# Two stacked cross-attention layers: where the last output projections stand, and in which order the first unit is set up

## The chip, the cores and the metric

The kernel runs on one core of one Trainium2 chip. The metric is the device time of one execution, in microseconds (us). A core has a matrix engine, TensorE (PE in the profile; its weight loads are the rows PEld), VectorE (DVE), ScalarE (ACT), GpSimd (POOL) and SyncE (SP). DMA transfers are issued by instructions on SP's and ACT's queues and run beside the engines. Matrix products go from SBUF to PSUM[...].

## The reference

x is 32 batches of 256 tokens with 320 channels, the context 32 batches of 77 tokens with 512 channels. Two layers run one after the other; each has 20 heads of 16 channels and adds its result to its input. The reference has more branches for context tokens beyond the 77th, but there are none, so each layer is, with weights and a bias of its own:

```python
q = heads(x @ wq); k = heads(ctx @ wk); v = heads(ctx @ wv)
p = softmax(q @ k.T / 4)          # over the 77 context tokens
x = x + merge(p @ v) @ wo + bias
```

Everything is float32.

## The kernel before

**Units.** Two batches make a pair; a *unit* is one pair in one layer, so there are 32 units. `units_in_order` starts layer 0 four pairs ahead of layer 1 and then alternates; the last four units are pairs 12 to 15 in layer 1. Data lie with channels on partitions: a tile of 128 x 1280 holds channels 0 to 127 and 128 to 255 of both batches (1024 columns) and, in the last 256 columns, the remaining 64 channels of both batches, one batch above the other. A unit is cut into five *groups* of heads and batches (`of_group`); groups 0 to 3 are a channel block and a batch, group 4 is the rest of both.

**Steps of a unit**, with the tile that the profile shows for each. Each product is written in column strips of 32 (`by_columns`, line 173).
- `keys`, `keys_rest` (psk, lines 230 and 248): context times key weights; ACT copies the result to kR (lines 245, 263), and `mask_keys` (line 219, POOL) makes two versions kT, one for each head of a pair. `less_keys` (line 226, POOL) makes kM, which also carries a row that subtracts the maximum.
- `queries`, `queries_rest` (psq, lines 266 and 278): x times query weights; ACT copies to q0 (lines 276, 284). `queries_rest` also issues a DMA that copies all of q0 to q1 (line 285, 640 KB).
- `maxima` (psm, line 335): query times key, only to get each row's maximum; DVE reduces four banks (line 343).
- `turn` (line 350): DVE transposes the maxima of all groups to mT, and eight small DMAs on SP's queue (line 356) write them into q0 and q1, into rows that belong to the other head. Scores then come out with the maximum subtracted.
- `scores` (pss, line 369), exponentials on ACT (pT, line 375, four of 590 ns a group).
- `values` (po, line 389): the numerators and, from columns of ones, the sums. DVE transposes (line 401) and takes reciprocals (405), POOL multiplies (410), DVE transposes back into oT (`turn_back`, line 424).
- `finish`, `finish_rest` (psy, lines 437 and 445): oT times output weights; `add` (line 431, DVE) adds bias and residual into the x tile. `main_channels` covers the 256 channels, `last_channels` the remaining 64; the rest is for output channels 256 to 319. In layer 1 the x tile is then stored (line 452; for the last unit group by group, line 435).
- `vals`, `place_vals` (psv, lines 293 and 311): values in chunks of 128 context rows, placed per unit by DMA (line 322).

**Order.** The order is written out by hand. `at(slot, where, step)` puts steps into *slots*, five per unit; unit u's scores stand in slots 5u to 5u + 4. Within a slot the order is load, maxima, turn, scores, values, rest, back, full, last (line 506). Unit u prepares itself beside the scores of the units before it: context loaded in slot 5u − 12, queries in 5u − 9, keys in 5u − 8, values from 5u − 6, maxima in 5u − 6 to 5u − 2, turn in 5u − 2; it finishes in 5u + 6 and 5u + 8 (lines 462 to 496). For the last two units `finish` and `finish_rest` stand in slots 159 and 160. Slots below 0 are the prologue. Every engine and every DMA queue keeps to the program's order; what waits for what is by semaphores. PSUM banks are handed out in rotation, eight of them, so a step waits for the reader of the bank that was handed out eight banks earlier.

**Prologue.** At the start SP's queue loads unit 0's context and then pair 0's x, ACT's queue the key weights and then the query weights of layer 0 (lines 134 to 137). TensorE's first step is `keys(0)`, then `queries(0)`.

Of the kernel before, what the change touches and what calls it, by code (L numbers as in the profile page):

```python
# [48 lines left out]
F32 = mybir.dt.float32  # L49
# [19 lines left out]
PARTS, WIDE = {}, 0  # L69
# [21 lines left out]
def xattn_kernel(ctx: ExitStack, tc: tile.TileContext, xT, cT, cP, weights, outT):  # L91
    nc = tc.nc
# [3 lines left out]
    work = ctx.enter_context(tc.tile_pool(name="work", bufs=3))  # L96
# [3 lines left out]
    units = units_in_order()  # L100
    NU = len(units)

    def bank(name):
        return psum.tile([P, 512], F32, tag="bank", name=name)

    xs, cs, cvs = {}, {}, {}

    def load_x(p):
        x_sb = io.tile([P, NX], F32, tag="x", name=f"x_{p}", bufs=AHEAD + 3)
        nc.sync.dma_start(out=x_sb, in_=xT[p])  # L110
        xs[p] = x_sb

    def load_context(u):
        p = units[u][0]
        c_sb = cs[u] = io.tile([P, NKA, NB * L], F32, tag="c", name=f"c_{u}", bufs=3)
        nc.sync.dma_start(out=c_sb, in_=cP[:, p])


    w_sb = []
# [7 lines left out]
    def load_weights(layer, first, last, queue):  # L127
        a = PARTS[first][0]
        at, rows, width = PARTS[last]
        b = at + rows * width  # L130
        queue.dma_start(out=w_sb[layer]["all"][:, a:b], in_=weights[layer][:, a:b])


    load_context(0)
    load_weights(0, "k", "k", nc.scalar)
    load_x(0)
    load_weights(0, "q", "q22", nc.scalar)

    ident = const.tile([P, P], F32, name="ident")
    make_identity(nc, ident)  # L140
# [19 lines left out]
    masks = const.tile([P, 2], F32, name="masks")  # L160
# [3 lines left out]
    for e in range(2):  # L164
        i = HD * (1 - e)
        nc.vector.tensor_scalar_mul(less[:, e : e + 1], r32[:, i : i + 1], -1.0)

    st = [{} for _ in units]

    def by_columns(out, lhsT, rhs, **flags):  # L170

        for m in range(0, out.shape[0], 32):
            nc.tensor.matmul(out[m : m + 32], lhsT[:, m : m + 32], rhs, **flags)  # L173
# [6 lines left out]

    def last_channels(ps, w2, x, **flags):
        for t in range(2):
            for b in range(NB):
                r = slice(64 * b, 64 * b + 64)
                by_columns(
                    ps[t][b][:, 0:S], w2[r, 0, t * P : (t + 1) * P], x[r, 2 * NT : NX], **flags
                )

    def main_channels(ps, w, x, start, stop):
        for t in range(2):
            for kc in range(2):
                for b in range(NB):
                    i = kc * NT + b * S
                    by_columns(
                        ps[t][b][:, 0:S], w[:, kc, t * P : (t + 1) * P], x[:, i : i + S],
                        start=(start and kc == 0), stop=(stop and kc == 1),
                    )

    def project_rest(ps, w, w22, x):

# [12 lines left out]
    def mask_keys(u, g0, g1):  # L215

        kR, kT = st[u]["kr"], st[u]["k"]
        for e in range(2):
            nc.gpsimd.tensor_scalar_mul(kT[:, e, g0:g1], kR[:, g0:g1], masks[:, e : e + 1])  # L219

    def less_keys(u):

# [43 lines left out]
    def queries(u):  # L266
        p, layer = units[u]
        w = w_sb[layer]
        q0, _ = st[u]["q"] = [
            work.tile([P, NX], F32, tag=f"q{e}", name=f"q{e}_{u}", bufs=3) for e in range(2)  # L270
        ]
        ps = [[bank(f"psq_{u}_{t}_{b}") for b in range(NB)] for t in range(2)]
        last_channels(ps, w["q2"], xs[p], start=True, stop=False)
        main_channels(ps, w["q"], xs[p], start=False, stop=True)
        for g in range(4):
            nc.scalar.copy(of_group(q0, g), ps[g // 2][g % 2][:, 0:S])  # L276

# [72 lines left out]
    def turn(u):  # L350
        mT = work.tile([P, 2 * NG * 32], F32, tag="mT", name=f"mT_{u}", bufs=2)
        nc.vector.transpose(mT, maxes[u % 2].rearrange("p k i -> p (k i)"))
        for e in range(2):
            q = st[u]["q"][e].rearrange("(j i) n -> i j n", i=32)[HD * (1 - e)]
            for a in range(P // 32):
                nc.sync.dma_start(  # L356
                    out=q.rearrange("j (k a n) -> a j k n", a=P // 32, n=32)[a],
                    in_=mT[32 * a + e : 32 * a + 8 : 2].rearrange("j (k n) -> j k n", n=32),
                )
# [17 lines left out]
    def products(u, g):  # L377
        vpad = st[u]["v"]
        if "o" not in st[u]:
            st[u]["o"] = work.tile([P, NX], F32, tag="oT", name=f"oT_{u}", bufs=2)  # L380
        po = bank(f"po_{u}_{g}")
        pT = st[u].pop(("p", g))
        for e in range(2):
            for j in range(4):
                if g < 4:
                    b, pair = g % 2, 4 * (g // 2) + j
                else:
                    b, pair = j // 2, 8 + j % 2
                nc.tensor.matmul(  # L389
                    po[32 * j : 32 * j + 32, e * S : (e + 1) * S],  # L390
                    vpad[:L, b, pair, e].rearrange("p a d -> p (a d)"),
                    pT[j][:L, e * S : (e + 1) * S],
                    start=True,
                    stop=True,
                )
        return po
# [21 lines left out]
    def values(u, g):  # L418
        st[u]["n", g] = divide(u, g, products(u, g))
# [7 lines left out]
    def add(u, g, ps):  # L427
        p, layer = units[u]
        x = of_group(xs[p], g)
        t = g // 2  # L430
        nc.vector.scalar_tensor_tensor(  # L431
            x, ps[:, 0:S], w_sb[layer]["b"][:, 0, t : t + 1], x, ALU.add, ALU.add
        )
        if u == NU - 1:
            nc.sync.dma_start(out=of_group(outT[p], g), in_=x)

    def finish(u):
        w = w_sb[units[u][1]]
        ps = [[bank(f"psy_{u}_{t}_{b}") for b in range(NB)] for t in range(2)]
        main_channels(ps, w["o"], st[u]["o"], start=True, stop=False)  # L440
        last_channels(ps, w["o2"], st[u]["o"], start=False, stop=True)
        for g in range(4):
            add(u, g, ps[g // 2][g % 2])

    def finish_rest(u):
        p, layer = units[u]
        w = w_sb[layer]
        ps = bank(f"psy_{u}_2")
        project_rest(ps, w["o"], w["o22"], st[u]["o"])
        add(u, 4, ps)  # L450
        if layer == 1 and u < NU - 1:
            nc.sync.dma_start(out=outT[p], in_=xs[p])
        st[u].clear()


    place = {}
# [1 line left out]
    def at(slot, where, step):  # L458
        place.setdefault((slot, where), []).append(step)

    made = [0, 0]
    for u, (p, layer) in enumerate(units):
        s = NG * u
        if layer == 0 and u > 0:
            at(s - 14, "load", lambda p=p: load_x(p))
        if u > 0:
            at(s - 12, "load", lambda u=u: load_context(u))
        at(s - 8 if u else s - 9, "rest", lambda u=u: keys(u))
        at(s - 9, "last", lambda u=u: queries(u))
        at(s - 7, "rest", lambda u=u: keys_rest(u))  # L470
# [12 lines left out]
        for g in range(NG):  # L483
            at(s - 6 + g, "maxima", lambda u=u, g=g: maxima(u, g))
# [3 lines left out]
        at(s - 2, "turn", lambda u=u: turn(u))  # L488
        if u < NU - 2:
            at(s + NG + 1, "full", lambda u=u: finish(u))  # L490
            at(s + NG + 3, "rest", lambda u=u: finish_rest(u))
        else:

            slot = NG * NU - (u == NU - 2)
            at(slot, "full", lambda u=u: finish(u))
            at(slot, "last", lambda u=u: finish_rest(u))


    at(-10, "load", lambda: load_weights(0, "v", "v", nc.scalar))
# [106 lines left out]
```

## Time and profile before

| | |
|---|---|
| time, median of 3 runs | 984.96 us (984.57 to 988.63) |
| the profiled execution's own time | 986.19 us |
| its span, first to last instruction | 984.4 us |
| TensorE busy | 968.2 us, 98% of the span |
| DVE, ACT, POOL busy | 566.7, 430.1, 240.9 us |
| DMA | 83.59 MB, mean 85 GB/s |
| mean granted TensorE clock | 0.995 |

A row of a timeline gives start, duration, engine, line and operation, written and read tiles, the shape, the count of instructions, and in brackets how long the engine had been idle before it and what ended that. A float32 product appears as two instructions, so a maxima step of 8 products is x16. Durations of grouped rows overlap with the next row, since products are pipelined; the distance from one start to the next is what a step takes. A row of a stretch gives its bounds, its length, the busy time and count of PE, PEld, DVE, ACT and POOL, then the granted TensorE clock (1.00 is full), the share of the DMA engines in use and GB/s.

### The profile page before, as it was taken

To read this page: it belongs to the slowest core of one execution; us is meant where nothing else is said; L and a number is where in the kernel's file an instruction comes from. 1 tells how busy PE (TensorE), PEld (TensorE's weight loads), DVE (VectorE), ACT (ScalarE), POOL (GpSimd) and SP (SyncE) were. 2 spreads that over 40 slices of the span, in tenths; PEclk is the share of its full clock that TensorE was granted. 3 is DMA by queue.
4 is the path that set the end of the run, shared out by engine and by line. 5 is a ranking of instruction groups with operands and counts; after the bars stand their busy time and mean duration, and the time that the engine had idled before them with its cause. 6 is when DMAs were issued, how large, how long until landed. Compare 5 with 4: busy or idle time off the path is not lost.

```text
span 984.4 us, 43943 instructions
## 1 busy us (share of the span) xinstructions
PE 968.2 (98%) x19664; PEld 597.3 (61%) x19664; DVE 566.7 (58%) x1316; ACT 430.1 (44%) x937; POOL 240.9 (24%) x364
## 2 busy tenths in 40 slices
PE   7899999999999999999999999999999999999988
PEld 4566665666665666665666666666656666656644
DVE  2466555665555655556655556655556655556554
ACT  1354444444444444444544444543444444444443
POOL 3132221322212322212312213322223222123211
PEclk9999999999999999999999999999999999999999
DMA  6450222212132311323212232311323122231111
GB/s 216 165 174 21 92 80 97 70 62 72 64 123 71 121 54 50 107 81 123 63 51 85 70 124 71 104 44 60 123 81 118 33 67 70 70 108 48 50 57 55
DMA packets 53949, 83.59 MB, mean 85 GB/s; under 512 B 15556, under 2 KB 35652, under 8 KB 53762
## 3 DMA queue, kind: packets, MB, share of 16 engines
q1 hardware_dynamic: 53330, 78.96, 24.0%
q8 instruction: 154, 2.52, 1.0%
q10 hardware_dynamic: 432, 1.84, 0.5%
q14 instruction: 33, 0.27, 0.1%
HBM read 35.39 MB, written 10.49 MB: 47 GB/s over the span
## 4 chain that ended last, share of the span: by engine, by line
PE 97%; DMA 1%; DVE 1%; SPq 1%; POOL 0%; issue 0%; ACT 0%; DVEq 0%; POOLq 0%
PE po L389 16%; PE psy L173 15%; PE psq L173 15%; PE pss L369 14%; PE psm L335 12%; PE psv L173 9%; PE psk L173 7%; PE psq L212 4%; PE psy L212 4%; PE psk L256 2%; SPq L356 1%; DMA w<-in_w_dram 1%; DVE max L343 0%; DMA q<-mT 0%; POOL kT L219 0%
## 5 line engine op out<-in xcount | busy, mean ns | idle before, releaser
L375 ACT ACTIVATE pT<-pss 77x512 f32<-77x512 f32 x640 | 326.8, 590 | 210.4 <-PE pss L369 210.4
L343 DVE TENSOR_REDUCE max<-psm 128x4 f32<-128x308 f32 x640 | 260.6, 469 | 197.4 <-PE psm L335 194.0
L410 POOL TENSOR_TENSOR normal<-turned,inv 128x256 f32<-128x256 f32 x160 | 99.2, 620 | 684.5 <-DVE inv L405 684.5
L369 PE MATMUL pss<-q,kM 32*77 32x256 f32 x2560 | 170.9, 377 | 4.5 <-DMA q<-mT 4.5
L389 PE MATMUL po<-pT,v 77*32 77x256 f32 x2560 | 173.1, 388 | 1.3 <-DVE max L343 1.3
L173 PE MATMUL psy<-oT,w 128*32 128x256 f32 (+1 forms) x3072 | 149.2, 380 | 0.0
L173 PE MATMUL psq<-x,w 128*32 128x256 f32 (+1 forms) x3072 | 149.2, 379 | 0.0
L276 ACT COPY q<-psq 128x256 f32<-128x256 f32 x128 | 47.6, 372 | 205.9 <-PE psq L173 202.1
L401 DVE STREAM_TRANSPOSE turned<-po 128x512 f32<-128x512 f32 x160 | 113.3, 708 | 38.4 <-PE po L389 35.4
L424 DVE STREAM_TRANSPOSE oT<-normal 128x256 f32<-128x256 f32 x160 | 71.3, 445 | 109.4 <-POOL normal L410 109.4
L335 PE MATMUL psm<-kT,q 32*128 32x154 f32 x2560 | 129.4, 314 | 1.2 <-POOL kT L219 1.2
L335 PEld LDWEIGHTS psm<-kT,q 32*128 32x128 f32 x2560 | 92.2, 183 | 57.0 <-issue 34.9
L389 PEld LDWEIGHTS po<-pT,v 77*32 77x32 f32 x2560 | 67.4, 109 | 89.9 <-DVE max L343 58.7
L173 PEld LDWEIGHTS psq<-x,w 128*32 128x32 f32 (+1 forms) x3072 | 85.4, 108 | 57.2 <-issue 13.6
L173 PEld LDWEIGHTS psy<-oT,w 128*32 128x32 f32 (+1 forms) x3072 | 82.2, 109 | 61.2 <-issue 13.2
L369 PEld LDWEIGHTS pss<-q,kM 32*77 32x77 f32 x2560 | 102.2, 142 | 24.5 <-issue 6.8
L219 POOL TENSOR_SCALAR kT<-kR,masks 128x77 f32<-128x77 f32 (+1 forms) x128 | 96.7, 766 | 50.9 <-ACT kR L245 41.3
L431 DVE SCALAR_TENSOR_TENSOR x<-psy,w,x 128x256 f32<-128x256 f32 x160 | 68.6, 479 | 61.2 <-PE psy L173 56.5
L173 PE MATMUL psv<-w,cv 128*32 128x320 f32 x1232 | 93.5, 433 | 0.0
L173 PE MATMUL psk<-c,w 128*32 128x154 f32 x2048 | 75.0, 298 | 5.8 <-DMA w<-in_w_dram 5.8
L173 PEld LDWEIGHTS psk<-c,w 128*32 128x32 f32 x2048 | 67.0, 111 | 12.9 <-DMA w<-in_w_dram 5.8
L173 PEld LDWEIGHTS psv<-w,cv 128*32 128x32 f32 x1232 | 41.1, 110 | 40.6 <-issue 2.2
(25 smaller groups left out, 349.1 us busy)
## 6 DMA issues: line engine op xcount, KB each, us to landing
q<-q SPq DMA_DIRECT2D x32, 640.0 KB
x<-in_xT_dram SPq DMA_DIRECT2D x16, 640.0 KB
c<-in_cP_dram SPq DMA_DIRECT2D x32, 308.0 KB
cv<-in_cT_dram SPq DMA_DIRECT2D x38, 256.0 KB
out_dram<-x SPq DMA_DIRECT2D x15, 640.0 KB
v<-stage SPq DMA_DIRECT2D x26, 192.5 KB
q<-mT SPq DMA_DIRECT2D x256, 5.0 KB
w<-in_w_dram ACTq DMA_DIRECT2D x2, 640.0 KB
```

What stands on the lines that cost most here:

```text
L173: nc.tensor.matmul(out[m : m + 32], lhsT[:, m : m + 32], rhs, **flags)
L212: nc.tensor.matmul(ps[r, 0:S], lhsT, rhs, start=(kc == 0), stop=(kc == 2))
L219: nc.gpsimd.tensor_scalar_mul(kT[:, e, g0:g1], kR[:, g0:g1], masks[:, e : e + 1])
L335: nc.tensor.matmul(ps[j][:, c * 2 * L : (c + 1) * 2 * L], q[r, c * P : (c + 1) * P], kT[r, :, g, :], start=True, stop=True,)
L343: nc.vector.tensor_reduce(mx[:, 2 * g : 2 * g + 2, 2 * j : 2 * j + 2], ps[j][:, : 4 * L].rearrange("p (c e k) -> p c e k", e=2, k=L), AX.X ...
L369: nc.tensor.matmul(ps[j][:L, e * S : (e + 1) * S], kM[r, e, g, :], q[r, :], start=True, stop=True,)
L375: nc.scalar.activation(st[u]["p", g][j][:L], ps[j][:L], AF.Exp, scale=SCALE)
L389: nc.tensor.matmul(po[32 * j : 32 * j + 32, e * S : (e + 1) * S], vpad[:L, b, pair, e].rearrange("p a d -> p (a d)"), pT[j][:L, e * S : (e ...
L401: nc.vector.transpose(turned[:, 0 : 2 * S], po)
L410: nc.gpsimd.tensor_tensor(normal.rearrange("p q e d -> p e q d"), outs, inv.unsqueeze(3).broadcast_to([P, 2, S // 32, HD]), ALU.mult,)
L424: nc.vector.transpose(of_group(st[u]["o"], g), normal)
L431: nc.vector.scalar_tensor_tensor(x, ps[:, 0:S], w_sb[layer]["b"][:, 0, t : t + 1], x, ALU.add, ALU.add)
```

## The change

In the tail, the output projections of units 28, 29 and 30 are held back. Each `finish` is split into two halves, one for each 128 output channels, and the halves and rests get slots of their own: unit 28 in 151, 152 and (rest) 148, unit 29 in 153, 154 and 155, unit 30 in 156, 159 and 157. A half uses two banks in place of four and runs the last channels first. The store of a unit follows its last part. Unit 31 finishes in slot 160 as before. oT gets three buffers in place of two.

In the prologue the loads of pair 0's x (in three pieces) and of the query weights (in three) come ahead of those of the context and the key weights, and TensorE's first step is `queries(0)` with the last channels last, then `keys(0)` and its rest. Ahead of it stand five products of the identity with itself, whose result nobody reads. Unit 0's key masks go from POOL to DVE. Unit 0's maxima stand in slots −6, −5, −4, −4 and −3, its turn in −3 with two of its eight DMAs on ACT's queue; keys and queries of unit 1 move to slots −4 and −3. Pair 1's x is loaded on ACT's queue.

```diff
+        if p == 0:
+            for a, b in ((0, NT), (NT, 2 * NT), (2 * NT, NX)):
+                nc.sync.dma_start(out=x_sb[:, a:b], in_=xT[p, :, a:b])
+        else:
+            (nc.scalar if p == 1 else nc.sync).dma_start(out=x_sb, in_=xT[p])
...
+    load_x(0)
+    first, _, _ = PARTS["q"]
+    for i in range(2):
+        n = slice(first + i * C, first + (i + 1) * C)
+        nc.scalar.dma_start(out=w_sb[0]["all"][:, n], in_=weights[0][:, n])
+    load_weights(0, "q2", "q22", nc.scalar)
     load_context(0)
     load_weights(0, "k", "k", nc.scalar)
-    load_x(0)
-    load_weights(0, "q", "q22", nc.scalar)
...
+    warm = bank("warm")
+    for _ in range(5):
+        nc.tensor.matmul(warm[:, 0:P], ident, ident, start=True, stop=True)
...
+    def main_channels(ps, w, x, start, stop, ts=(0, 1)):
+        for t in ts:
+            steps = [(kc, b) for kc in range(2) for b in range(NB)]
+            if len(ts) == 1:
+                steps.sort(key=lambda step: step[1])
...
+        engine = nc.gpsimd if u else nc.vector
         for e in range(2):
-            nc.gpsimd.tensor_scalar_mul(kT[:, e, g0:g1], kR[:, g0:g1], masks[:, e : e + 1])
+            engine.tensor_scalar_mul(kT[:, e, g0:g1], kR[:, g0:g1], masks[:, e : e + 1])
...
+                queue = nc.scalar if u == 0 and a == 3 else nc.sync
+                queue.dma_start(
...
-            st[u]["o"] = work.tile([P, NX], F32, tag="oT", name=f"oT_{u}", bufs=2)
+            st[u]["o"] = work.tile([P, NX], F32, tag="oT", name=f"oT_{u}", bufs=3)
...
+    def finish(u, ts=(0, 1)):
         w = w_sb[units[u][1]]
+        ps = {t: [bank(f"psy_{u}_{t}_{b}") for b in range(NB)] for t in ts}
+        if len(ts) == 1:
+            last_channels(ps, w["o2"], st[u]["o"], start=True, stop=False, ts=ts)
+            main_channels(ps, w["o"], st[u]["o"], start=False, stop=True, ts=ts)
+        else:
+            main_channels(ps, w["o"], st[u]["o"], start=True, stop=False)
+            last_channels(ps, w["o2"], st[u]["o"], start=False, stop=True)
+        for t in ts:
+            for b in range(NB):
+                add(u, 2 * t + b, ps[t][b])
...
+    end = NG * NU
+    late = {
+        NU - 4: (end - 9, end - 8, end - 12),
+        NU - 3: (end - 7, end - 6, end - 5),
+        NU - 2: (end - 4, end - 1, end - 3),
+    }
...
+        at(late[u][2] if u in late else s + NG + 3, "rest", lambda u=u: finish_rest(u))
+        if u not in late:
             at(s + NG + 1, "full", lambda u=u: finish(u))
+            continue
+        for t in range(2):
+            at(late[u][t], "full", lambda u=u, t=t: finish(u, (t,)))
+        at(max(late[u]), "last", lambda u=u: store(u))
+
+    at(-10, "last", lambda: queries(0))
+    at(-9, "rest", lambda: keys(0))
+    at(-9, "rest", lambda: keys_rest(0))
+    for slot, g in ((-6, 0), (-5, 1), (-4, 2), (-4, 3), (-3, 4)):
+        at(slot, "maxima", lambda g=g: maxima(0, g))
+    at(-3, "turn", lambda: turn(0))
+    at(-4, "rest", lambda: keys(1))
+    at(-4, "rest", lambda: keys_rest(1))
+    at(-3, "last", lambda: queries(1))
```

More of the change, by code (lines that the diff above doesn't have):

```diff
@@ L109, in load_x @@
         x_sb = io.tile([P, NX], F32, tag="x", name=f"x_{p}", bufs=AHEAD + 3)
-        nc.sync.dma_start(out=x_sb, in_=xT[p])
         xs[p] = x_sb
+        if p == 0:
[3 more added lines that the diff above has]
+            (nc.scalar if p == 1 else nc.sync).dma_start(out=x_sb, in_=xT[p])
     def load_context(u):
@@ L179, in of_group, with last_channels @@
         return x[:, 2 * NT : NX]
-    def last_channels(ps, w2, x, **flags):
-        for t in range(2):
+    def last_channels(ps, w2, x, ts=(0, 1), **flags):
+        for t in ts:
             for b in range(NB):
@@ L189, in last_channels @@
                 )
[L191 to L199, printed above, removed]
+    def main_channels(ps, w, x, start, stop, ts=(0, 1)):
[3 more added lines that the diff above has]
+                steps.sort(key=lambda step: step[1])
+            for kc, b in steps:
+                i = kc * NT + b * S
+                by_columns(
+                    ps[t][b][:, 0:S], w[:, kc, t * P : (t + 1) * P], x[:, i : i + S],
+                    start=(start and kc == 0), stop=(stop and kc == 1),
+                )
     def project_rest(ps, w, w22, x):
@@ L272, in queries @@
         ps = [[bank(f"psq_{u}_{t}_{b}") for b in range(NB)] for t in range(2)]
-        last_channels(ps, w["q2"], xs[p], start=True, stop=False)
-        main_channels(ps, w["q"], xs[p], start=False, stop=True)
+        if u == 0:
+            main_channels(ps, w["q"], xs[p], start=True, stop=False)
+            last_channels(ps, w["q2"], xs[p], start=False, stop=True)
+        else:
+            last_channels(ps, w["q2"], xs[p], start=True, stop=False)
+            main_channels(ps, w["q"], xs[p], start=False, stop=True)
         for g in range(4):
@@ L355, in turn @@
             for a in range(P // 32):
-                nc.sync.dma_start(
+                queue = nc.scalar if u == 0 and a == 3 else nc.sync
+                queue.dma_start(
                     out=q.rearrange("j (k a n) -> a j k n", a=P // 32, n=32)[a],
@@ L435, in add, with store @@
             nc.sync.dma_start(out=of_group(outT[p], g), in_=x)
-    def finish(u):
+    def finish(u, ts=(0, 1)):
         w = w_sb[units[u][1]]
[L439 to L443, printed above, removed]
+        ps = {t: [bank(f"psy_{u}_{t}_{b}") for b in range(NB)] for t in ts}
+        if len(ts) == 1:
+            last_channels(ps, w["o2"], st[u]["o"], start=True, stop=False, ts=ts)
+            main_channels(ps, w["o"], st[u]["o"], start=False, stop=True, ts=ts)
+        else:
+            main_channels(ps, w["o"], st[u]["o"], start=True, stop=False)
+            last_channels(ps, w["o2"], st[u]["o"], start=False, stop=True)
+        for t in ts:
+            for b in range(NB):
+                add(u, 2 * t + b, ps[t][b])
+    def store(u):
+        p, layer = units[u]
+        if layer == 1 and u < NU - 1:
+            nc.sync.dma_start(out=outT[p], in_=xs[p])
+        st[u].clear()
     def finish_rest(u):
@@ L450, in finish_rest @@
         add(u, 4, ps)
-        if layer == 1 and u < NU - 1:
-            nc.sync.dma_start(out=outT[p], in_=xs[p])
-        st[u].clear()
+        if u not in late:
+            store(u)
     place = {}
@@ L467, in xattn_kernel @@
             at(s - 12, "load", lambda u=u: load_context(u))
-        at(s - 8 if u else s - 9, "rest", lambda u=u: keys(u))
-        at(s - 9, "last", lambda u=u: queries(u))
-        at(s - 7, "rest", lambda u=u: keys_rest(u))
+        if u > 1:
+            at(s - 8, "rest", lambda u=u: keys(u))
+            at(s - 9, "last", lambda u=u: queries(u))
+            at(s - 7, "rest", lambda u=u: keys_rest(u))
         need = range(p * NB * L // P, ((p + 1) * NB * L - 1) // P + 1)
@@ L483, in xattn_kernel @@
         for g in range(NG):
-            at(s - 6 + g, "maxima", lambda u=u, g=g: maxima(u, g))
+            if u > 0:
+                at(s - 6 + g, "maxima", lambda u=u, g=g: maxima(u, g))
             at(s + g, "scores", lambda u=u, g=g: scores(u, g))
@@ L487, in xattn_kernel @@
             at(s + g + 1, "back", lambda u=u, g=g: turn_back(u, g))
-        at(s - 2, "turn", lambda u=u: turn(u))
-        if u < NU - 2:
-            at(s + NG + 1, "full", lambda u=u: finish(u))
[L491 to L496, printed above, removed]
+        if u > 0:
+            at(s - 2, "turn", lambda u=u: turn(u))
+        if u == NU - 1:
+            at(s + NG, "full", lambda u=u: finish(u))
+            at(s + NG, "last", lambda u=u: finish_rest(u))
+            continue
+        at(late[u][2] if u in late else s + NG + 3, "rest", lambda u=u: finish_rest(u))
+        if u not in late:
+            at(s + NG + 1, "full", lambda u=u: finish(u))
+            continue
+        for t in range(2):
[10 more added lines that the diff above has]
+    at(-3, "last", lambda: queries(1))
     at(-10, "load", lambda: load_weights(0, "v", "v", nc.scalar))
```

## The prediction

> **What bounds the kernel now.** I read the page's part 4 first (the chain that ended last), then TensorE's timeline in the middle, at both ends, and the stretches with their granted clock. All numbers are µs.
>
> The chain is TensorE almost alone:
>
> ```profile
> PE 97%; DMA 1%; DVE 1%; SPq 1%; POOL 0%; issue 0%; ACT 0%; DVEq 0%; POOLq 0%
> ```
>
> So a gain must come from time in which TensorE waits or runs at a low clock. To find it I need what each step costs when TensorE is fed. TensorE's timeline in the middle gives that as the distance from one start to the next:
>
> ```profile
> 528.35 0.81 PE L335 MATMUL psm<-kT,q 32*128 32x154 f32 x16
> 528.99 1.04 PE L369 MATMUL pss<-q,kM 32*77 32x256 f32 x16
> 529.96 1.07 PE L389 MATMUL po<-pT,v 77*32 77x256 f32 x16
> 530.84 2.29 PE L173 MATMUL psk<-c,w 128*32 128x154 f32 x64
> ...
> 548.66 4.66 PE L173 MATMUL psy<-oT,w 128*32 128x256 f32 x96
> 553.12 3.15 PE L173 MATMUL psq<-x,w 64*32 64x256 f32 x68
> ```
>
> A maxima step (psm) costs 0.64, scores (pss) 0.97, values (po) 0.88, an output projection (psy) 4.46. The same view gives psk 2.22 and its rest 0.65, psq 4.6 and its rest 1.4, psv 2.27, psy's rest 1.29. In the middle nothing is lost, and the change leaves it alone. The ends lose much. The last slots in TensorE's timeline:
>
> ```profile
> 936.75 4.66 PE L173 MATMUL psy<-oT,w 128*32 128x256 f32 x96
> ...
> 952.95 0.67 PE L369 MATMUL pss<-q,kM 32*77 32x256 f32 x8 [1.00 <-DMA q<-mT]
> 955.35 1.15 PE L369 MATMUL pss<-q,kM 32*77 32x256 f32 x8 [1.72 <-DMA q<-mT]
> 956.42 1.93 PE L389 MATMUL po<-pT,v 77*32 77x256 f32 x16
> ...
> 979.49 1.50 PE L212 MATMUL psy<-oT,w 128*32 128x256 f32 x24
> ```
>
> From 936.75 to 980.99 are 44.2. Fed, the work is 3 psy (13.4), 3 rests (4.1), 2 psm (1.3), 8 pss (7.8), 9 po (7.9): 34.5. **Lost in the tail: 9.7.** Only 3.5 of it shows as idle brackets; the rest is the half clock (the po of 1.93 instead of 1.07) and slots too thin to hide ScalarE's four exponentials (2.04 a slot). The granted clock, the column behind the busy times, shows it:
>
> ```profile
> 40.00:41.00 1.00, 1.00 (x14) 0.40 (x12) 0.00 (x0) 0.77 (x2) 0.00 (x0) 0.57 0.60 179
> 955.00:956.00 1.00, 0.65 (x8) 0.38 (x8) 0.00 (x0) 0.00 (x0) 0.00 (x0) 0.50 1.00 415
> ```
>
> The prologue, TensorE's timeline from 0:
>
> ```profile
> 5.76 4.07 PE L173 MATMUL psk<-c,w 128*32 128x154 f32 x64 [5.76 <-DMA w<-in_w_dram]
> 9.75 4.68 PE L173 MATMUL psq<-x,w 64*32 64x256 f32 x96
> 14.90 0.81 PE L335 MATMUL psm<-kT,q 32*128 32x154 f32 x16
> ...
> 33.24 0.81 PE L335 MATMUL psm<-kT,q 32*128 32x154 f32 x16 [1.18 <-POOL kT L219]
> ...
> 39.55 0.67 PE L369 MATMUL pss<-q,kM 32*77 32x256 f32 x8 [1.57 <-DMA q<-mT]
> ...
> 43.81 1.03 PE L369 MATMUL pss<-q,kM 32*77 32x256 f32 x16
> ```
>
> The first psk takes 4.0 where it later takes 2.22: half clock, although the clock column says 1.00 here. Idle before the first product 5.76, later 1.18, 0.23 and 1.57, then half clock from 40 to 43.6.
>
> **The change, part by part.** *Start of the prologue, up to the first psm (14.90 now).* The first step now needs the first third of x (256 KB) and one weight slice (160 KB) instead of 308 + 640 KB. In 0.5 µs stretches the transfers begin at 1.5, have moved 0.2 MB by 3.0 and then run at 400 GB/s. 416 KB are through at 3.55; the 948 KB of now would have been through at 4.85 but landed at 5.71, so up to 0.86 more: data at 3.6 to 4.4. But five identity products stand ahead of it on TensorE. They need the identity (VectorE had it at 1.85), so start near 1.95. No row shows a product over the whole array. Below: a psm step runs two rounds of 154 columns in 0.74 when alone, 0.37 each; by columns that is 0.31 for 128, at half clock 0.62, so 3.1 for five, end 5.0. If none of the weight load is exposed, streaming alone, some 2.1, gives 4.1; if both loads of a product (183 ns each, doubled by the clock) stand bare, 6.8 gives 8.7. I take 5.2, nearest to psm, whose loads are partly hidden. The data are there by then.
>
> When does the clock rise? By the row, 4.0 after the first product (5.76 to 9.75), so at 5.95. The Trainium skill, "TensorE: Matmul & The Clock Gate", Part 1, speaks of a free-running window of 3.4 that has to be busy: an estimate from it is 5.4 to 8.8, since a window already begun at 1.95 may not count. By the row psq ends at 5.95 + 4.6 − 0.4 (what was done at half speed) = 10.15; by the page's late end 11.5. I take the row and keep 1.4 for the range. Keys' bytes (2.3 MB with what shares the queues) are through by 8.1 to 8.9, before 10.15, so hidden by psq; if psq ended at 9 they would cost nothing yet. Then psk 2.2, its rest 0.65: 13.0. The masks are now on VectorE right in front of psm: copy 0.29 and two masks. The old ones took 1.05 each on GpSimd; the nearest VectorE row, 128x256, is 0.48. From psk's end 0.4 + two of 0.2 to 0.45, of which 0.65 lies beside psk's rest: a new wait of 0.15 to 0.65; I take 0.5. First psm at 13.5: **gain 1.4** (−0.5 to 2.5). Behind the masks VectorE holds only psm's own reductions.
>
> *From the first psm to the second unit-0 pss (14.90 to 43.81, 28.9 now).* In the new order TensorE has 8 psm (5.9, alone 0.74 each), 3 psv (6.8), 2 psq rests (2.75), psq 4.6, psk 2.25, its rest 0.65, one pss (1.0): 24.0. Does every wait go? The keys of unit 1 now stand two slots ahead of their psm, so GpSimd's 3.0 of masks lie under psm and psq. The turn follows unit 0's last psm; from that psm's start come the reductions and transpose (3.0 in the middle of the trace), then the 8 small DMAs at 0.58 (4.7) and 1.65 to land: 9.35; with two on ScalarE's queue 1.15 less, 8.2. TensorE meanwhile has psm, psq, psm, psv, psm = 9.1, so scores find it landed. ScalarE's queue waits for the transpose with unit 1's query copies behind it: it is released some 3.1 after that psm, the first psq bank is ready about 3, so the copies slip by about 1 and no one needs them before psq ends. On SP's queue c for unit 2 now stands behind the turn; it is needed four slots later. The big q copy is issued 9 ahead of the turn; it took about 4 here. Two psm groups side by side need eight banks; reductions (0.41 each) free them before psk and psm come round. Remaining loss 0.1. **Gain 4.8** (3 to 5).
>
> *Tail.* The number of matmuls, additions and stores is the same; three oT buffers only allow the later reads. Slots 151 to 154 and 156, 159 get half a projection (2.23), 155 and 157 a rest (1.29). Fed slots then last 4.7 (to 153), 4.1, 3.15: above ScalarE's 2.04. What is late next: (a) the last unit's turn. Psm in slot 153 waits on VectorE behind the additions of the half before it: turn landed 9.7 after psm's start; slots 153 and 154 hold 4.7 + 4.1 = 8.8, and the second half of the scores needs it 0.5 later: wait 0.4. The store of unit 28 is now ahead of the turn on SP's queue, but its addition ends 2 before the transpose. (b) Slot 158 gets nothing: 1.85 against 2.04, and 159's values want exponentials begun 2.8 earlier that need 2.7: 0.5. (c) Six half projections, whose second addition frees a bank that a pss needs at once: about 0.15 each, 0.9. (d) 0.2 more. Left: 2.0. **Gain 7.7** (4 to 8.7). Unit 28's work was in slot 146 beside psq; without it that slot still holds 7.1.
>
> Here a rule speaks against part of this: the same page, "HAM oscillation", says that only an idle gap beyond some 3.4 lowers the clock. The rows differ: gaps of 1.00 and 1.72 with 0.67 of work between, and the clock is 0.50 from 954.95 to 961.6, which costs half of 6.3. By the rule that 3.1 had another cause that may stay, and the tail's gain would be 4.6; by the row it goes with the gaps. The measurement decides; the 0.81 gap at 947 lowered nothing, so 0.4 is safe.
>
> **Sum.** 1.4 + 4.8 + 7.7 = 13.9 against the profiled execution, 986.2 (span 984.4 and 1.8 around it): 972.3. That execution is 1.2 above the median of 984.96, from which the same gain gives 971.1. I forecast 971.7.
>
> **Rivals.** *R1: the tail fills only half* (0.15). Adding halves lengthens VectorE's queue in front of pss and the turn; for it speaks slot 152 now, a pss of 1.78 behind four additions. Gain 10.0: about 975.5. *R2: the start is not faster* (0.12): identity products too long, a late clock, or late keys, and half of the 4.8 lost to a new wait before psm or scores. Gain 10.1: 975.5. Both together (0.03): about 979. *R3, slower* (0.04): the clock stays at half through the prologue because pieces arrive one by one and TensorE stutters. Place: 5.95 to the first scores; price: half of that time. It would have to eat 13.9, so half clock until about 34, against 9.75 now; until 40 it would cost 17, giving 988. Against it: the products queued behind each wait, 9.1 of them between turn and scores alone, with no transfer among their inputs that is not long due. The likeliest case has 0.66.
>
> **Chances.** What a measurement here can tell from no change is about 0.5%, 4.9. R1, R2 and the main case are all below 980; their bounds (0.5 of the masks, 1.4 of the clock, 1.7 of a longer identity run; 3 more if everything at the start lands early) give 967.5 to 978.5. Faster 0.92, same 0.04, slower 0.04.
>
> **What would show it.** After: first psq near 5.2, first psm near 13.5, second unit-0 pss near 37.5; no q<-mT wait above 0.5; clock 1.00 after 6; from the psy half in slot 151 on, po and pss near 1.07 throughout; in the middle the same 29.35 a unit (553.12 to 582.47 now, one psq to the next). Wrong if the identity products end after 6, if a new idle bracket above 1 µs stands before psm, or if the last unit's scores still wait for the turn.

## The result and the profile after

The changed kernel takes **974.41 us** (median of 4 runs, 974.11 to 974.99); the kernel before took 985.69 beside it (4 runs, 984.57 to 988.63). The ratio is 0.988 (95% interval 0.986 to 0.991). The forecast was 971.7, with a range of 967.5 to 978.5. The profiled execution of the changed kernel took 974.26 with a span of 972.5, against 986.19 and 984.4.

Part 4 of the page after, the chain that ended last, is now TensorE alone:

```profile
PE 99%; DVE 1%; POOL 0%; issue 0%; ACT 0%; POOLq 0%
```

I cut both traces at the same four events. All numbers are us.

| stretch | before | after | gain | predicted |
|---|---|---|---|---|
| start to the first psm | 14.90 | 13.97 | 0.93 | 1.4 |
| first psm to the second pss of unit 0 | 28.91 | 23.93 | 4.98 | 4.8 |
| that pss to the values in slot 146 | 862.74 | 863.14 | −0.40 | 0 |
| those values (906.55, now 901.04) to the end of the last product | 74.44 | 68.09 | 6.35 | 7.7 |
| behind the last product | 3.41 | 3.37 | 0.04 | 0 |
| span | 984.4 | 972.5 | 11.9 | 13.9 |

**Prologue.** TensorE's timeline after, from 0 to the second unit-0 pss:

```profile
1.88 2.50 PE L179 MATMUL warm<-ident 128*128 128x128 f32 x10 [1.88 <-POOL ident masks.py:199]
4.37 6.16 PE L186 MATMUL psq<-x,w 128*32 128x256 f32 x96
10.46 2.31 PE L186 MATMUL psk<-c,w 128*32 128x154 f32 x64
...
13.97 0.81 PE L357 MATMUL psm<-kT,q 32*128 32x154 f32 x16 [0.67 <-DVE kT L236]
...
31.18 0.81 PE L357 MATMUL psm<-kT,q 32*128 32x154 f32 x16 [0.27 <-issue]
31.92 2.36 PE L186 MATMUL psv<-w,cv 128*32 128x320 f32 x32
34.21 0.81 PE L357 MATMUL psm<-kT,q 32*128 32x154 f32 x16
34.84 1.07 PE L392 MATMUL pss<-q,kM 32*77 32x256 f32 x16
...
37.90 1.44 PE L392 MATMUL pss<-q,kM 32*77 32x256 f32 x16
```

The identity products took 2.50, so psq starts at 4.37. It then takes 6.09 instead of the fed 4.6: 1.5 too long, and since work at half clock takes twice its time, 3.0 of it ran at half clock, until about 7.4. Late data are not the reason: in the trace, groups of four products start 0.43 apart without a gap up to 7.38, and 0.22 apart from there on. The clock column does not show the half clock. The row of the stretch from 2 to 8 after (the granted clock is third from the end):

```profile
2.00:8.00 6.00, 6.00 (x50) 3.86 (x54) 0.54 (x4) 1.28 (x1) 2.15 (x5) 1.00 0.98 344
```

What the trace stores of the clock begins only with the rise, at 7.41; ahead of it the column prints 1.00. So in the first microseconds the clock has to be read from durations or from that first entry. The scores at 34.84 have no bracket: the turn's waits are gone. The small bracket at 31.18 is new, and the step from 37.90 to the next start (39.26) is 1.36 instead of 0.97. ScalarE's timeline after explains both:

```profile
28.65 2.02 ACTq L379 DMA_DIRECT2D q<-mT  x2
30.71 1.20 ACT L298 COPY q<-psq 128x256 f32<-128x256 f32 x4 [4.86 <-DMA q<-mT]
...
35.89 2.05 ACT L398 ACTIVATE pT<-pss 77x512 f32<-77x512 f32 x4 [1.12 <-PE pss L392]
37.82 0.38 ACT L306 COPY q<-psq 128x256 f32<-128x256 f32 x1
```

The two turn DMAs hold ScalarE for 2.02, and the four query copies of unit 1, which free banks, come after them. Later one query copy stands behind four exponentials, and the second pss finds its fourth bank free only at 38.2.

**Tail.** TensorE's timeline after, at the first half projection, at the last unit's scores and at the end:

```profile
926.03 1.07 PE L412 MATMUL po<-pT,v 77*32 77x256 f32 x16
927.03 2.53 PE L186 MATMUL psy<-oT,w 64*32 64x256 f32 x48
929.49 0.81 PE L357 MATMUL psm<-kT,q 32*128 32x154 f32 x16
930.12 1.20 PE L392 MATMUL pss<-q,kM 32*77 32x256 f32 x16
931.25 1.07 PE L412 MATMUL po<-pT,v 77*32 77x256 f32 x16
...
944.42 1.10 PE L392 MATMUL pss<-q,kM 32*77 32x256 f32 x16
945.45 1.07 PE L412 MATMUL po<-pT,v 77*32 77x256 f32 x16
...
967.63 1.50 PE L228 MATMUL psy<-oT,w 128*32 128x256 f32 x24
```

No wait for the turn is left, and pss and po stay near their fed durations, where before they took up to 2.00. The stretch row after shows full clock and a TensorE that never stops, in what was the disturbed region:

```profile
940.00:950.00 10.00, 10.00 (x176) 4.92 (x184) 4.76 (x12) 5.16 (x11) 1.24 (x2) 1.00 0.12 38
```

But a half projection takes 2.46 from start to start (927.03 to 929.49) instead of 2.23, the values ahead of it 1.00 instead of 0.88, and the pss behind it 1.13 instead of 0.97.

The list of TensorE's waits after is complete in four rows (total, count, longest):

```profile
PE warm L179 <- POOL ident masks.py:199: 1.9, 1, 1.9
PE psm L357 <- DVE kT L236: 0.7, 1, 0.7
PE po L412 <- DVE max L365: 0.5, 1, 0.5
PE psm L357 <- issue: 0.3, 1, 0.3
```

### The profile page after: what moved, and what is told of

It is laid out like the page before. It is cut to its first block, busy times and chain, and to the rows that moved or that the text cites. A ratio compares the mean times of both kernels' runs of the same rounds, so it can differ in the third digit from the quotient of the medians.

```text
span 972.5 us, 43974 instructions
## 1 busy us (share of the span) xinstructions
PE 965.8 (99%) x19674; PEld 597.1 (61%) x19674; DVE 567.6 (58%) x1320; ACT 430.2 (44%) x937; POOL 238.8 (25%) x360
## 4 chain that ended last, share of the span: by engine, by line
PE 99%; DVE 1%; POOL 0%; issue 0%; ACT 0%; POOLq 0%
PE po L412 16%; PE psq L186 15%; PE psy L186 15%; PE pss L392 14%; PE psm L357 12%; PE psv L186 9%; PE psk L186 7%; PE psq L228 4%; PE psy L228 4%; PE psk L273 2%; PE warm L179 0%; DVE max L365 0%; DVE kT L236 0%; POOL stage L156 0%; POOL normal L433 0%
## 5 line engine op out<-in xcount | busy, mean ns | idle before, releaser
L392 PE MATMUL pss<-q,kM 32*77 32x256 f32 x2560 | 168.6, 374 | 0.0
L236 POOL TENSOR_SCALAR kT<-kR,masks 128x308 f32<-128x308 f32 (+1 forms) x124 | 93.9, 769 | 38.6 <-ACT kR L262 32.0
```

The costliest lines, as they stand in the source:

```text
L236: engine.tensor_scalar_mul(kT[:, e, g0:g1], kR[:, g0:g1], masks[:, e : e + 1])
L392: nc.tensor.matmul(ps[j][:L, e * S : (e + 1) * S], kM[r, e, g, :], q[r, :], start=True, stop=True,)
```

## The experiments

Theory: two independent gains, about 6 in the prologue and 6 to 8 in the tail, and in the tail two causes together, slots too thin to fill TensorE and the half clock that the turn's gaps bring. Rivals: one part does all the work; the half clock has another cause than the gaps; a weaker filling of the tail would have done as well. Diffs are against the changed kernel unless said. Ratios are to the kernel before on the same chip, with 95% intervals. The kernel before scatters there (single runs from 984.5 to 992.7), the changed one hardly, so the variants are compared by their times and traces as well.

### The tail alone, the prologue alone

The tail alone: the prologue functions as before (loads, order, masks on POOL, the turn on SP's queue alone, no identity products).

```diff
...
-        if u > 1:
-            at(s - 8, "rest", lambda u=u: keys(u))
...
+        at(s - 8 if u else s - 9, "rest", lambda u=u: keys(u))
...
-    at(-10, "last", lambda: queries(0))
-    at(-9, "rest", lambda: keys(0))
...
```

> Only the tail of the change, the prologue as before. My theory: the two halves of the gain are independent, so the stretch from slot 146's values to TensorE's last product takes 68.1 us as in the changed kernel (74.4 before), the prologue is as before (second unit-0 scores near 43.8), and the time is about 979.3. Rival: the tail's gain needs the other banks or queues of the new prologue; then the stretch is above 69.

Measured: 979.67 (979.36 to 979.86), ratio 0.989 (0.987 to 0.991). Its second unit-0 pss starts at 43.41 (43.81 before). From slot 146's values to the last product it takes 68.08, the changed kernel 68.09.

The prologue alone: no held-back projections, the last two units finish in 159 and 160 as before.

```diff
-    late = {
-        NU - 4: (end - 9, end - 8, end - 12),
-        NU - 3: (end - 7, end - 6, end - 5),
-        NU - 2: (end - 4, end - 1, end - 3),
-    }
+    late = {}
...
```

> Only the prologue of the change, the last projections as before. My theory: second unit-0 scores at 37.9 as in the changed kernel, the stretch from slot 146's values to the last product 74.4, the half clock and the two waits for the last unit's turn are back, time about 980. Rival: the earlier start is partly given back in the middle, then the time is above 981.

Measured: 984.12 (981.9 to 985.64), ratio 0.993 (0.991 to 0.995). That is 4 more than I expected, and not by the rival: the second unit-0 pss is at 37.32, so the whole gain of the start is there, and the middle, 863.5, is only 0.4 longer than in the changed kernel. The tail takes 77.2 against 74.44 in the profile of before. TensorE's timeline of this kernel:

```profile
947.37 0.67 PE L392 MATMUL pss<-q,kM 32*77 32x256 f32 x8 [1.10 <-DMA q<-mT]
949.56 1.15 PE L392 MATMUL pss<-q,kM 32*77 32x256 f32 x8 [1.52 <-DMA q<-mT]
950.64 1.93 PE L412 MATMUL po<-pT,v 77*32 77x256 f32 x16
952.50 2.01 PE L392 MATMUL pss<-q,kM 32*77 32x256 f32 x16
...
960.10 2.00 PE L392 MATMUL pss<-q,kM 32*77 32x256 f32 x16
962.03 1.07 PE L412 MATMUL po<-pT,v 77*32 77x256 f32 x16
```

and stretches in the half clock, around its start and around its end:

```profile
952.00:956.00 4.00, 4.00 (x40) 1.49 (x32) 1.42 (x3) 2.22 (x5) 0.62 (x1) 0.50 0.01 4
948.29:948.39 0.10, 0.00 (x0) 0.00 (x0) 0.10 (x1) 0.00 (x0) 0.00 (x0) 1.00 0.07 12
948.39:948.49 0.10, 0.00 (x0) 0.00 (x0) 0.10 (x1) 0.00 (x0) 0.00 (x0) 0.50 0.24 37
961.94:962.04 0.10, 0.10 (x5) 0.01 (x1) 0.00 (x1) 0.00 (x0) 0.07 (x1) 0.50 0.00 0
962.04:962.14 0.10, 0.10 (x8) 0.10 (x8) 0.10 (x1) 0.00 (x0) 0.00 (x0) 0.98 0.00 0
```

The two gaps are nearly those of before (1.10 and 1.52 against 1.00 and 1.72), but the half clock lasts from 948.39 to 962.04, 13.65, where the profile of before had 6.83 (954.90 to 961.73). From 952 on TensorE is 100% busy in it and does half the work. In all fourteen traces every stretch between two changes of the clock is a whole multiple of 3.41: one of them at half clock in the prologue of before, two and four of them in these tails. What follows: the two parts are independent, since the new tail takes the same with the old prologue (68.08 and 68.09), and the new prologue gains as much with the old tail. And the price of the gaps differs from execution to execution, which the profile of before, one execution, could not show. The granted clock of the single runs of the kernel before does: 0.998 in those of 984.5 and 984.6, 0.995 to 0.997 around 986.4, 0.993 around 988.6, 0.990 or 0.991 around 990.6, 0.988 from 991.9 to 992.7.

### What the half clock costs

The kernel *before*, with ten identity products, read by nobody, in slot 154, where TensorE waits for the last turn:

```diff
+    def fill():
+        ps = bank("fill")
+        for _ in range(10):
+            nc.tensor.matmul(ps[:, 0:P], ident, ident, start=True, stop=True)
+
+    at(NG * NU - 6, "last", fill)
```

> The kernel before, with ten identity products (read by nobody, about 2.5 of TensorE) at the end of slot 154, where it waits for the last unit's turn. The work and the wait for the turn are otherwise as before. If the half clock comes from the gaps of 1.0 and 1.7, it goes: po and pss of slots 155 to 157 take 1.07 and 1.10, and the time falls by half of what was run at half clock, 3 in the profiled execution of before, to about 983 on a chip where before is 986, with less scatter. If gaps this short do not lower the clock, the clock column still shows 0.50 and the time is unchanged.

Measured: 983.25 (982.99 to 983.66, 6 runs), ratio 0.9955 (0.993 to 0.998). Its timeline at the turn:

```profile
951.91 2.50 PE L502 MATMUL fill<-ident 128*128 128x128 f32 x20
954.34 0.67 PE L369 MATMUL pss<-q,kM 32*77 32x256 f32 x8
955.37 0.67 PE L369 MATMUL pss<-q,kM 32*77 32x256 f32 x8 [0.36 <-DMA q<-mT]
955.97 1.07 PE L389 MATMUL po<-pT,v 77*32 77x256 f32 x16
```

and the stretch behind it:

```profile
955.00:960.00 5.00, 4.64 (x74) 2.39 (x72) 2.05 (x4) 3.89 (x8) 0.62 (x1) 1.00 0.32 128
```

Useless products change only what the gap does to the clock: it stays at 1.00, po is 1.07. The median falls by 5.2 (988.43 beside it; by the interval 2.4 to 6.5), and the scatter, 7.7 before, shrinks to 0.7. So the gaps do lower the clock, and how long it then stays low is what made single runs of the kernel before differ. In the trace the stretch from slot 146's values to the last product takes 71.66, against 74.44 before and 77.2 with the prologue alone. From here to the kernel with the whole new tail are 3.6 more, in the trace (68.08) and in the medians (979.67, in other runs): that is what useful work in the slots adds, since the wait for the turn still costs this kernel 2.8, most of it filled with useless products, and the slots behind it stay thin.

### How the tail is filled

Whole projections of units 28 to 30 in slots 152, 154 and 157 instead of six halves:

```diff
-        NU - 4: (end - 9, end - 8, end - 12),
-        NU - 3: (end - 7, end - 6, end - 5),
-        NU - 2: (end - 4, end - 1, end - 3),
+        NU - 4: (end - 8, end - 12),
+        NU - 3: (end - 6, end - 5),
+        NU - 2: (end - 3, end - 4),
...
```

> The changed kernel with whole projections in place of halves: unit 28 in slot 152 (rest 148), unit 29 in 154 (rest 155), unit 30 in 157 (rest 156). My theory: a half costs 0.23 more than half of a whole and its values step up to 0.11 more, from the change of step and not from the order inside; three wholes save about 1.0 to 1.8, and give back about 0.65 at each scores step behind four additions, so the stretch from slot 146's values to the last product is 68.1 give or take 0.7 and the time 973.7 to 975. Rival: halves are what makes the tail work; then scores and the turn wait again and the time is 976 or more.

Measured: 975.94 (975.01 to 976.4), ratio 0.9885 (0.986 to 0.991); the last stretch takes 69.66, 1.6 more than with halves. Between the two expectations, nearer to the rival. Its timeline shows both ways to lose:

```profile
927.54 1.70 PE L392 MATMUL pss<-q,kM 32*77 32x256 f32 x16
929.71 1.07 PE L412 MATMUL po<-pT,v 77*32 77x256 f32 x16 [0.47 <-DVE max L365]
930.60 4.66 PE L186 MATMUL psy<-oT,w 128*32 128x256 f32 x96
...
935.82 1.85 PE L392 MATMUL pss<-q,kM 32*77 32x256 f32 x16
```

An empty slot leaves TensorE in front of ScalarE and VectorE, and behind a whole projection a pss waits for banks that four additions free one after the other. Halves give less of either.

Then why is a half dearer than half of a whole? Two variants change the order inside it: channels 0 to 255 first and the last 64 behind them, as in the whole projection, and the new sort by batch left out.

```diff
-        if len(ts) == 1:
-            last_channels(ps, w["o2"], st[u]["o"], start=True, stop=False, ts=ts)
-            main_channels(ps, w["o"], st[u]["o"], start=False, stop=True, ts=ts)
...
+        main_channels(ps, w["o"], st[u]["o"], start=True, stop=False, ts=ts)
+        last_channels(ps, w["o2"], st[u]["o"], start=False, stop=True, ts=ts)
```

> The changed kernel, but each half projection does the 256 main channels first and the last 64 after them, as a whole projection does. My theory: the tail falls short because a step that begins with 64-row products after values costs 0.11 before it and 0.13 to 0.23 in it, six times; then a half takes 2.25 in place of 2.46 from start to start, values to half 0.88 in place of 1.00, and the time falls by 1.5 to 2, to about 972.6. Rival: the cost lies in halving itself (two banks, a bank's two products back to back), then nothing changes, 974.4.

```diff
-            if len(ts) == 1:
-
-                steps.sort(key=lambda step: step[1])
```

> The changed kernel, but a half projection takes its two channel blocks in the order of a whole one (block by block, both banks in turn) instead of bank by bank; the last 64 channels stay first. If a bank's products back to back cost something, a half falls from 2.46 towards 2.36 and the time by up to 0.6. If the order bank by bank is what frees the first bank early, a half stays at 2.46 and the scores behind it wait 0.2 to 0.3 more in the two slots that still have maxima: time up by 0.5. I expect the second.

Measured: 974.07 (973.49 to 974.95), ratio 0.983 (0.981 to 0.985), and 974.24 (973.38 to 974.3), ratio 0.985 (0.981 to 0.989). From the values ahead of the first half to the last product the changed kernel takes 43.10, the first variant 43.02, the second 43.10. Main channels first gives 0.11 back ahead of the half (values to half 0.89) and loses it behind the two halves that maxima follow (pss 1.42 instead of 1.13, as both banks are complete only at the end); the half itself stays at 2.44. Both my expectations of a loss or a gain by order were wrong. The traces show where the cost sits. Inside a projection, whole or half, groups of four products start 0.22 apart, but 0.33 where the products change between 128 and 64 input rows, and 0.33 again at the end, where psm or pss with 32 rows follow. A whole projection has one such change inside, and so has each half; and each half has another at its end. Values, with 77 rows, take 0.88 ahead of products of 128 rows and 1.00 ahead of 64. So the cost belongs to the splitting: each change in the number of rows costs about 0.11, and six halves have twice as many as three wholes. A whole psy followed by a psm costs 4.59 where followed by psq, which begins with 64 rows, it is 4.46. No run varied the row counts alone.

### The pieces of the prologue

Without the identity products:

```diff
-    warm = bank("warm")
-    for _ in range(5):
-        nc.tensor.matmul(warm[:, 0:P], ident, ident, start=True, stop=True)
```

> The changed kernel without the five identity products. By the row of before (clock up 4.0 after the first product) queries begin at 4.37 and run at half clock to 8.4 in place of 7.4: first maxima 0.5 later, time 974.9. If the clock follows a window that does not start with the products, no change. If the products were worth what they are for, half clock until 10 and first maxima 1.3 later.

Measured: 974.74 (974.2 to 975.19), ratio 0.984 (0.982 to 0.985). Its first psq:

```profile
4.58 6.89 PE L183 MATMUL psq<-x,w 128*32 128x256 f32 x96 [4.58 <-DMA w<-in_w_dram]
```

The data land at 4.58, so the products ran in time that was free anyway. Psq takes 6.82, half clock until 9.0 instead of 7.4, the first psm is at 14.91 and the second unit-0 pss at 38.85 (37.90 with them). In the trace the products bring 0.9; in the medians the ranges of the two do not quite separate that from nothing.

Unit 0's masks back on POOL:

```diff
-        engine = nc.gpsimd if u else nc.vector
+        engine = nc.gpsimd
```

> The changed kernel with unit 0's key masks on GpSimd as before the change. Masks of 1.05 each instead of about 0.27: the wait in front of the first maxima grows from 0.67 to about 2.2, everything after it is 1.5 later, time about 975.9. If instead the wait was for the copy or the semaphores, it stays below 1.2 and the time below 975.

Measured: 976.39 (976.04 to 976.82), ratio 0.989 (0.987 to 0.991):

```profile
15.60 0.81 PE L357 MATMUL psm<-kT,q 32*128 32x154 f32 x16 [2.07 <-POOL kT L236]
```

The wait is 2.07 instead of 0.67, so the engine of the masks is worth 1.4 of the time directly ahead of the first psm. In this execution psq also began 0.6 later, at 4.99. This gap of 2.07 did not lower the clock: the psv behind it takes its usual 2.29. On the grid of 3.41 counted from that trace's rise (7.25) one step ends inside the gap, at 14.07, and no step has more than 1.53 of idle time.

The turn of unit 0 on SP's queue alone:

```diff
-                queue = nc.scalar if u == 0 and a == 3 else nc.sync
+                queue = nc.sync
```

> The changed kernel with all eight DMAs of unit 0's turn on SP's queue. My theory: the 0.27 that TensorE waits before unit 1's first maxima comes from ScalarE being held by its two DMAs to 30.7, so it goes; the last DMA then lands near 34.8, when the second half of the scores wants it at 35.0, so no new wait or at most 0.2: time 974.2. Rival: the queue split is needed, scores wait 0.5 or more as they did before the change, time 974.9.

Measured: 974.12 (973.78 to 974.95), ratio 0.987 (0.985 to 0.989). SP issues all eight in 4.74, from 28.91, and the scores still find them landed; the 0.27 at 31.18 is gone:

```profile
26.57 4.68 PE L186 MATMUL psq<-x,w 64*32 64x256 f32 x96
31.19 0.81 PE L357 MATMUL psm<-kT,q 32*128 32x154 f32 x16
...
34.85 1.11 PE L392 MATMUL pss<-q,kM 32*77 32x256 f32 x16
```

From psm of group 4 to the second pss 12.11 instead of 12.41: 0.3 in the trace, too little for the medians. The two DMAs on ScalarE's queue are a small loss, not a gain.

The first psm behind the first psv, to hide the wait for the masks:

```diff
-    for slot, g in ((-6, 0), (-5, 1), (-4, 2), (-4, 3), (-3, 4)):
+    for slot, g in ((-5, 0), (-5, 1), (-4, 2), (-4, 3), (-3, 4)):
```

> The changed kernel with unit 0's first maxima moved one slot, behind the first chunk of values. The 0.67 that TensorE waits for VectorE's masks is then covered by 2.3 of values, if their weights have landed by 13.3: second unit-0 scores 0.7 earlier, time 0.7 lower. If the value weights are late, the wait only changes its name and nothing is gained.

Measured: 974.11 (973.83 to 974.28), ratio 0.985 (0.980 to 0.989). The 0.67 is gone, but psv takes 3.06 (12.95 to 16.01) instead of 2.29, with a stall from 14.3 to 14.8 that no wait explains. Nothing is gained.

Seven products of a tile of ones, set by VectorE, in place of five of the identity, so that TensorE starts at 1.03:

```diff
+    ones = const.tile([P, P], F32, name="ones")
+    nc.vector.memset(ones, 1.0)
...
-    for _ in range(5):
-        nc.tensor.matmul(warm[:, 0:P], ident, ident, start=True, stop=True)
+    for _ in range(7):
+        nc.tensor.matmul(warm[:, 0:P], ones, ones, start=True, stop=True)
```

> The changed kernel with seven products of a tile of ones (written by VectorE at the start) in place of five of the identity, so that they can begin near 0.7 instead of 1.88 and still end when the first data land near 4.4. In the profiles so far the clock rose 4.4 to 5.8 after the first product with them and at 8.7 to 9.3 on the time axis without. If it is the time of being busy that counts, it rises 1.2 earlier, queries take 5.0 to 5.4 instead of 5.5 to 6.3, time 0.6 lower. If the rise is tied to something else, nothing changes.

Measured: 973.69 (973.46 to 974.45), ratio 0.985 (0.981 to 0.988). Psq takes 5.29, half clock until 6.1, and the first psm is at 13.56; the profiled execution loses the rest again before its second pss (38.16).

Three of these edits together, the turn on one queue, psm behind psv and the early products:

> The changed kernel with the last two edits and the turn's DMAs all on SP's queue. If the three are independent the time is 1.3 to 1.7 lower than the changed kernel's, 972.7 to 973.1, with no idle bracket of TensorE between the first query product and slot 1 above 0.1. With two maxima steps side by side VectorE's reductions fall behind by one step; if that makes the turn late, scores wait and half of the gain is gone.

Measured: **973.40** (972.62 to 973.82), ratio 0.984 (0.980 to 0.988), the fastest of all. Its timeline:

```profile
1.03 3.36 PE L181 MATMUL warm<-ones 128*128 128x128 f32 x14 [1.03 <-DVE ones L148]
4.32 4.96 PE L188 MATMUL psq<-x,w 128*32 128x256 f32 x96
...
13.53 1.53 PE L188 MATMUL psv<-w,cv 128*32 128x320 f32 x17 [0.40 <-issue]
...
36.28 1.39 PE L394 MATMUL pss<-q,kM 32*77 32x256 f32 x16
```

Psq is down to 4.89 and the second unit-0 pss is 1.6 earlier than in the changed kernel, with a span of 970.8. On the same chip it is 0.8 below the changed kernel with another order in the halves (974.24), 0.7 below the run with psm behind psv alone and 0.3 below that with the early products alone; the ranges still touch. It is less than I expected, 972.7 to 973.1 without a bracket above 0.1: the 0.40 at 13.53 is new.

That stall and those of the two runs before have one place in common. Each stands directly behind TensorE's 221st recorded product instruction, whichever step that is: in psv in the first and the last, in the middle of psm in the second, which reads no value weights. So late value weights do not explain it. In each trace a transfer of 16 KB on a queue of instructions ended 1.3 to 1.5 before the stall did (13.44, 13.21 and 12.25 against 14.80, 14.66 and 13.53). That speaks for late instructions; no run moved them, so it is not shown.

## Why the prediction held, and where its sizes were off

The direction and both mechanisms held: the parts are independent, and the tail's half clock went with its gaps. Of the 2.7 between 971.7 and 974.4, 2.0 are terms of the sum (13.9 against 11.9). The other 0.6 is how I stood the sum to the median: I took the forecast below 972.3, because the median of three was below the profiled execution. More runs of the kernel before had medians of 985.7 to 990.7, so the profiled execution was no slow one. How large the gain is depends on how long the kernel before stays at half clock: the changed kernel is 10 below its fastest single run and 18 below its slowest. That the profile I reckoned from was near the fast end was chance.

- **Start, 1.4 predicted, 0.93 measured.** The identity products cost 2.5, not 3.2: 0.25 for each instruction, nearest to that end of my bounds at which no weight load is bare. So psq started 0.8 earlier than I put it. But the step "I take the row" failed. I took the clock to rise 4.0 after the first product, at 5.95, as in the row of before; it rose at 7.41, 5.5 after. The row itself I had misread: 4.0 is the whole first psk, and in that trace the clock rose at 9.41, 3.65 after the first product. The estimate from the rule of the Trainium skill, "TensorE: Matmul & The Clock Gate", Part 1, was 5.4 to 8.8, and holds here; the multiples of 3.41 in the traces agree with the free-running window that it rests on. In all traces the clock rose at the end of the first such window in which TensorE was idle for 0.61 or less; busy times of up to 2.43 in an earlier one did not do. That is 3.0 to 4.5 after the first product in four kernels without identity products, 4.4 to 5.8 in eight with five of them, 3.5 and 5.1 in the two that start at 1.03: it depends on where the window stands, and one row of it was no rate. Psq ended at 10.46, 0.3 after the forecast. The masks' wait was 0.67; I took 0.5 and had 0.65 as the upper bound.
- **From the first psm to the second pss, 4.8 and 4.98.** Every large wait went, as argued: 1.18, 0.23 and 1.57, and with them the 3.41 at half clock, which cost 1.7. The new order of these slots has no run of its own. "The copies slip by about 1 and no one needs them" was wrong by 0.27: the two DMAs held ScalarE for 2.02, and the run with all eight on SP took that wait away.
- **A term that was missing, 0.40.** The second pss waits for a bank whose reader, a query copy on ScalarE, stands behind four exponentials. I looked at queues for the turn and not for banks.
- **Tail, 7.7 and 6.35; left over 2.0 predicted, 3.5 measured** (68.09 less fed work of 64.6). The half clock's share went, as the row said. The rule in "HAM oscillation" of the same page names idle gaps beyond some 3.4; I read it as if only these lowered the clock, and that does not hold here: with 1.0 to 1.1 and 1.5 to 1.7 around 0.67 of work it fell in before and in the kernel with the new prologue alone, and with the gap filled it did not. (a) The turn's wait, 0.4, was nothing, by luck: slots 153 and 154 lasted 9.71, since their steps were longer than I took them, which is (c). (b) 0.5 for the last slots was about 0.3. **(c) is the mis-sized term**: 0.15 a half. Measured, a half is 0.23 longer than half a whole (the last one 0.11), the values ahead of it 0.12, and behind two of them the pss 0.16: 5 × 0.23 + 0.11 + 6 × 0.12 + 2 × 0.16 = 2.3 instead of 0.9. I had priced the bank wait behind a half, which is the 0.16, and not the splitting itself. The remaining 0.9 is spread over pss and rests that are 0.06 and 0.12 longer than in the middle, and other steps.
- **The rivals.** R1, a tail that fills only half, did not happen; whole projections, which come nearer to it, cost 1.6. R2's late clock happened in part, but its keys and scores did not wait. R3, half clock into the scores, did not: psk at 10.46 already takes its fed time.

Left open: what decides about a window of 3.41. The clock fell behind windows with 1.45, 1.8 and 2.28 of idle time and stayed behind those with up to 1.18, but also behind the 1.53 of the run with the masks on POOL, so idle time alone does not decide; and in the run with the prologue alone it stayed at half through two windows without any. Open too is what holds TensorE behind its 221st product instruction.

## What to carry to other kernels

Where TensorE waits twice within a few microseconds, look at the durations behind the waits: here two traces have idle brackets of 2.7 and 2.6, and the clock behind them cost 2.8 and 5.5, which ten useless products in the gap took away. When work is held back to fill thin slots, charge every extra change in the number of rows (0.11 here) and look at the banks of the step behind it; small pieces still won over whole ones by 1.6. In a prologue, put the smallest transfer that feeds a long product first (here its data landed at 4.58 instead of 5.76), and start TensorE on anything early, for it ran at half clock for 3 to 6 after its first product.

## What I had not expected of the hardware

- The granted clock changes only in steps of 3.41, and the half clock behind nearly the same two gaps lasted two of them in one profiled execution (6.83) and four in another (13.65). With the gaps filled or gone, the single runs of a kernel lie within 0.5 to 1.5, where the kernel before had 984.5 to 992.7.
- A single gap of 2.07 early on, with a step of that grid inside it, did not lower the clock.
- The granted clock in the profile reads 1.00 in the first 7.4 us, while products take up to twice their fed time.
- A float32 product of 128x128x128 took 0.5 at half clock (five in 2.49) and 0.24 at full clock (ten in 2.43).
- A change between products of 128, 64 and 32 rows costs about 0.11.
- Two small DMAs on ScalarE's queue held it for 2.02, where eight on SP's took 4.74, 0.59 each.
